# Four convolution layers in one kernel: the stores of x2 move from SyncE's DMA queue to GpSimd's

## The chip, the cores and the metric

One core of one Trainium2 chip runs the whole kernel. The metric is the device time of one execution in microseconds; 2562.26 is the median of three runs before the change.

The core's engines each run their own list of instructions in order: TensorE (PE, matrix products into PSUM), VectorE (DVE), ScalarE (ACT), GpSimd (POOL) and SyncE (SP). A DMA is issued by an engine's list, here SP's or POOL's, and then runs beside the engines. An instruction that waits holds up everything behind it in its own list.

## The reference

The input x is 16 images of 64 channels of 128 x 128 float32. Four layers follow each other, and each adds to its input what it makes of the input's group norm (32 groups of two channels, over the image):

```
x = x + L0(gn(x))    # gram = xf xf^T / N per image; y = gram xf; 1x1 convolution
x = x + L1(gn(x))    # Scharr: |horizontal 3x3| + |vertical 3x3|, each channel for itself
x = x + L2(gn(x))    # a quarter of the channels one column left, a quarter right; 3x3 conv; + b
x = x + L3(gn(x))    # 3x3 conv, 1x1 conv, batch norm over all images, leaky relu, clip to 0..255
```

In the kernel's names x2 is the result of L1's line, the input of the third layer; x3 is the result of L2's line; y is what L3's convolutions give ahead of the batch norm. The batch norm needs sums over all 16 images, so y or x3 of every image is kept in DRAM and the output is made in a second pass.

## The kernel before

**Tiles.** An image lies in SBUF as 128 partitions: 64 channels times two halves of the rows. It is worked in NS = 8 chunks of R = 8 rows for each half. The constants and the order are at lines 16 to 82.

**Stages of an image.** `Gram` (line 557) reads the image by columns (`xr` tiles, 512 KB a load, on SP), copies it on ACT into `xw` and makes the Gram matrix on PE; a chain of small steps (`gram_chain`, line 387) gives the mixing matrix `abd`. `Front` (line 624) loads x (`load`, line 639: one half on SP's queue, one on POOL's), multiplies it by `abd` on PE into `po`, writes the normalized rows with ACT into `xh` (three chunks in turn), and makes the Scharr layer in `scharr` (line 736). `Layer2` (line 889) loads x2 back with the shifted columns into `v` tiles (`load`, line 897: even rows on SP's queue, odd rows on POOL's, six to twelve DMAs a chunk), normalizes them in place on ACT (`norm`, line 957), takes the row differences on DVE into `dA` or `dB`, and multiplies on PE into the PSUM pair `two`, which DVE empties into x3 (`combine`, line 1022). `Layer3` (line 1042) does the like from x3 to y. The x3 and y stores are on SP's queue (lines 884 and 1123). For odd chunks POOL also copies half of `dB` to the tile `q2` with two DMAs (line 939).

**The x2 tile and its buffers.** `scharr` writes in place: the tile `u` (line 739, tag "u", two buffers from the pool `work`) becomes the x2 chunk after six parts, named in `SCHARR` (line 24): "stencil", "smooth", "slope", "abs" (ACT), "x +" and "+ y". The first DVE instruction of a chunk, the one in "stencil", overwrites the buffer of the chunk two before. So it has to wait until that chunk has been read by its store and by ACT's square sum (line 727).

**The store.** `Front.store` (line 766) writes a chunk of x2 to the DRAM tensor `x2_d` in two DMAs, one for the even and one for the odd rows of each half. Each takes 128 partitions x 4 rows x 128 values: 512 pieces of 512 bytes, 256 KB. Both are issued by `sp`. It is called in the part "x2" of the next chunk's step (line 724). The eighth chunk's store is what the next stage's first `v` load of the same image waits for.

**Order.** A step handles one chunk of `Front` and one pair of chunks of `Layer2` or `Layer3`; several images are in work at a time. Inside a step the parts come in the order of the table `ORDER` (line 27), one list for each kind of step. `InOrder` (line 124) keeps the instructions in program order, so each engine's list is the table written out. In SP's list a pair of x2 stores stands between loads of `v`, x and `xr` and stores of x3 and y. POOL's list has its halves of the x and `v` loads, the `q2` copies, the small steps of the norm coefficients (`rstd`, line 340, and `coefficients`, line 356), a few memsets (lines 715 and 720) and, at the end, the stores of the output.

**Semaphores.** The framework gives each kind of queue eight completion semaphores in turn. A DMA waits for the one eight before it on its queue to have landed.

**The second pass.** From about 2010 us no x2 is made any more: y or x3 is loaded, the batch norm applied, and the output stored (lines 1351 to 1456).

Of the kernel before, what the change touches and what calls it, by code (L numbers as in the profile page):

```python
# [170 lines left out]
def tile_kernel(ctx: ExitStack, tc: tile.TileContext, x, cw_h, w2_t, b2, wbin_t, w1_t, b1, gamma, beta, consts, out):  # L171
    nc = tc.nc
    pe, dve, act, sp, pool = (InOrder(tc, e) for e in (nc.tensor, nc.vector, nc.scalar, nc.sync, nc.gpsimd))
# [38 lines left out]
    def planes(d):  # L212

        return d[W:W + 2 * C * PLANE].rearrange("(p s j w) -> p s j w", s=2, j=NP // 2, w=W)
# [409 lines left out]
    class Front:  # L624
# [141 lines left out]
        def store(self, i):  # L766
            d = planes(x2_d[self.b])
            for s in range(2):
                sp.dma_start(
                    d[:, s, i * R // 2:(i + 1) * R // 2, :],  # L770
                    self.x2[i].rearrange("p (j s) w -> p s j w", s=2)[:, s],
                )
# [722 lines left out]
```

## Time and profile before

| | |
|---|---|
| runs | 2562.26 us median of 3 (2558.72 to 2563.32) |
| profiled execution | 2563.73 us, of which 2562.0 is the span from the first to the last instruction |
| granted TensorE clock | 0.976 in the mean |
| HBM | 321.46 MB read, 243.28 MB written |
| DMAs issued by SP | 58.0% of 16 DMA engines' time, 425.34 MB |
| DMAs issued by POOL | 20.1%, 156.63 MB |
| x2 stores | 256 DMAs of 256 KB on SP's queue, 4.9 us from issue to landing (median of those whose landing is known) |
| x loads | 128 DMAs of 256 KB on each queue, 4.5 us to landing from SP, 4.9 from POOL |
| one DMA on POOL's engine | `v` loads 503 ns, `q2` copies 524, x loads 602, output stores 537 to 549 |

How to read the profile: it shows one execution. [...] A group of instructions is named "out<-in" by the tiles it writes and reads, buffer numbers left out; so `x_d<-u` is a store of x2, `x_d<-x` a store of x3, and `v<-x_d` a load of x2. All lines are 134 because a helper records each instruction. The time in brackets is the idle time of the engine just before an instruction, with what released it. "SPq" is SP's list. The PSUM pair is `two`, the stencil's tile `u`.

### The profile page before, as it was taken

The page shows a single profiled execution, that of the slowest core. Times are in us where ns is not written, and L with a number is a line of the kernel's source. Part 1 is how long each engine was busy: PE and PEld are TensorE (multiplying, and loading weights), DVE is VectorE, ACT ScalarE, POOL GpSimd, SP SyncE. Part 2 cuts the span into 40 slices and gives each one's busy share as a digit, 9 for nine tenths or more (in the row PEclk, how much of TensorE's full clock was granted, in tenths as well). Part 3 has the DMA queues.
Part 4 walks back from the last instruction along what each step waited for, and adds up shares of the span by engine and source line. Part 5 has one row for each costly group of instructions (what it writes and reads, how often), then busy time and mean ns, then how long its engine had stood idle before and what let it go on. Part 6 is the DMA issues. An engine that isn't in the chain of part 4 may idle for free. (4 is left out here: it accounts for less than half of the span.)

```text
span 2562.0 us, 52738 instructions
## 1 busy us (share of the span) xinstructions
PE 2425.1 (95%) x19286; PEld 938.8 (37%) x19286; DVE 2120.4 (83%) x2939; ACT 2029.4 (79%) x3253; POOL 698.8 (27%) x1254
## 2 busy tenths in 40 slices
PE   6587999999999999999999999999999999999996
PEld 5332333333333333434343434343333333333332
DVE  4999999999999999999999999999999634444333
ACT  4777888889797979797978888887888655787775
POOL 3241313131313132323232323232321310222222
PEclk8688999999999999999999999999999999999998
DMA  9776979796767676757576979776767688999998
GB/s 228 194 195 180 233 199 233 192 233 188 191 171 193 163 197 160 201 160 201 160 199 173 243 192 231 200 205 168 200 170 193 156 264 261 417 417 417 413 412 338
DMA packets 610577, 585.33 MB, mean 228 GB/s; under 512 B 48480, under 2 KB 521984, under 8 KB 610320
## 3 DMA queue, kind: packets, MB, share of 16 engines
q1 hardware_dynamic: 556752, 425.34, 58.0%
q0 software_dynamic: 53568, 156.63, 20.1%
q8 instruction: 153, 2.51, 0.4%
q14 instruction: 104, 0.85, 0.1%
HBM read 321.46 MB, written 243.28 MB: 220 GB/s over the span
## 5 line engine op out<-in xcount | busy, mean ns | idle before, releaser
L134 PE MATMUL two<-dA,w 64*64 64x512 f32 (+2 forms) x2304 | 533.9, 595 | 0.0
L134 PE MATMUL two_again<-v_again,w 64*64 64x508 f32 (+1 forms) x3456 | 376.6, 592 | 10.7 <-ACT v_again L134 10.7
L134 POOL DMA_DIRECT2D v<-x_d x480 | 238.8, 503 | 499.8 <-PE one L134 220.3
L134 PE MATMUL one<-v,w 128*64 128x508 f32 (+2 forms) x1600 | 360.8, 584 | 0.3 <-ACT c L134 0.3
L134 PE MATMUL one<-v,wi 128*64 128x508 f32 (+3 forms) x1536 | 346.8, 585 | 13.6 <-ACT c L134 13.5
L134 PE MATMUL two<-dB,w 64*64 64x512 f32 (+2 forms) x1536 | 353.5, 593 | 0.0
L134 DVE SCALAR_TENSOR_TENSOR e<-e 128x1032 f32<-128x1032 f32 (+1 forms) x256 | 313.4, 1224 | 0.0
L134 ACT ACTIVATE xh<-po,co 128x128 f32<-128x128 f32 (+1 forms) x480 | 274.1, 619 | 13.3 <-PE po L134 12.4
L134 PEld LDWEIGHTS two<-dA,w 64*64 64x64 f32 (+1 forms) x2304 | 148.9, 133 | 276.9 <-issue 269.3
L134 ACT ACTIVATE junk<-x 128x1024 bf16<-128x1024 f32 x128 | 134.9, 1054 | 117.0 <-DVE x L134 116.5
L134 PEld LDWEIGHTS two_again<-v_again,w 64*64 64x64 f32 x3456 | 131.7, 134 | 254.7 <-issue 227.9
L134 ACT ACTIVATE v<-v,co 128x1154 f32<-128x1154 f32 x128 | 171.8, 1343 | 60.7 <-DMA v<-x_d 58.9
L134 ACT ACTIVATE v<-x,co 128x1024 f32<-128x1024 f32 (+3 forms) x256 | 205.0, 846 | 3.8 <-POOL co L134 3.8
L134 PE MATMUL po<-x,abd 64*64 64x512 f32 (+1 forms) x1024 | 183.3, 621 | 23.7 <-ACT xh L134 18.4
L134 DVE SCALAR_TENSOR_TENSOR u<-xh 128x1170 f32<-128x1170 f32 x128 | 176.0, 1375 | 34.5 <-DMA x_d<-u 28.1
L134 DVE SCALAR_TENSOR_TENSOR y<-two,c 128x1024 f32<-128x1024 f32 x128 | 156.0, 1219 | 52.4 <-issue 20.6
L134 DVE TENSOR_TENSOR dB<-v 128x1024 f32<-128x1024 f32 (+1 forms) x128 | 152.1, 1188 | 39.8 <-ACT v L134 31.9
L134 PEld LDWEIGHTS one<-v,w 128*64 128x64 f32 x1600 | 107.5, 137 | 206.2 <-issue 170.1
L134 PEld LDWEIGHTS one<-v,wi 128*64 128x64 f32 x1536 | 102.8, 136 | 215.7 <-issue 159.4
L134 ACT ACTIVATE junk<-y 128x1024 bf16<-128x1024 f32 x128 | 135.1, 1055 | 55.0 <-DVE y L134 53.7
L134 PE MATMUL two<-q,cross 64*64 64x512 f32 (+1 forms) x768 | 169.6, 570 | 6.3 <-issue 5.7
L134 PE MATMUL two<-dA,wi 128*64 128x508 f32 (+1 forms) x768 | 175.0, 589 | 0.0
(228 smaller groups left out, 4253.5 us busy)
## 6 DMA issues: line engine op xcount, KB each, us to landing
x_d<-u SPq DMA_DIRECT2D x256, 256.0 KB, 4.9
x_d<-x SPq DMA_DIRECT2D x490, 128.0 KB, 3.7
xr<-in_x SPq DMA_DIRECT2D x120, 512.0 KB, 6.2
y_d<-y SPq DMA_DIRECT2D x320, 128.0 KB, 3.8
x<-in_x SPq DMA_DIRECT2D x128, 256.0 KB, 4.5
x<-in_x POOLq DMA_DIRECT2D x128, 256.0 KB, 4.9
end_x<-x_d SPq DMA_DIRECT2D x36, 512.0 KB, 17.5
xw<-x_d SPq DMA_DIRECT2D x33, 512.0 KB, 17.2
```

Of the source, the lines that this page charges most:

```text
L134: return self.tc.keep_in_program_order(call(*args, **kwargs))
```

## The change

The two DMAs of each x2 chunk are issued by POOL's list instead of SP's. They stand at the same place of the program, in the part "x2"; shape, source and destination are as before. 256 DMAs go from one list to the other.

```diff
@@ -766,7 +766,7 @@
         def store(self, i):
             d = planes(x2_d[self.b])
             for s in range(2):
-                sp.dma_start(
+                pool.dma_start(
                     d[:, s, i * R // 2:(i + 1) * R // 2, :],
                     self.x2[i].rearrange("p (j s) w -> p s j w", s=2)[:, s],
                 )
```

## The prediction

> **What bounds the kernel now.** I read the engines' shares and the forty slices first, to find the stages.
>
> ```profile
> PE 2425.1 (95%) x19286; PEld 938.8 (37%) x19286; DVE 2120.4 (83%) x2939; ACT 2029.4 (79%) x3253; POOL 698.8 (27%) x1254
> ...
> PE   6587999999999999999999999999999999999996
> ...
> POOL 3241313131313132323232323232321310222222
> ```
>
> PE is full from the fifth slice (256 us) on, and POOL is never busier than four tenths. Then I cut the run where each image's eighth x2 chunk is finished on DVE, and asked for busy times: ten images together (380.28 to 1644.26), image 9 alone, image 13 alone.
>
> ```profile
> core 0: us, PE busy (x) PEld busy (x) DVE busy (x) ACT busy (x) POOL busy (x), PEclk, DMA share, GB/s
> 380.28:1644.26 1263.98, 1241.91 (x9844) 487.89 (x9842) 1215.89 (x1711) 1074.25 (x1792) 366.00 (x656) 1.00 0.74 194
> 1139.50:1265.81 126.31, 124.18 (x988) 48.79 (x986) 121.58 (x172) 107.42 (x181) 37.10 (x66) 1.00 0.69 181
> 1644.26:1768.58 124.32, 123.08 (x988) 48.49 (x986) 121.49 (x173) 102.41 (x176) 35.89 (x65) 1.00 0.69 183
> ```
>
> In the ten images PE idles 1263.98 - 1241.91 = 22.1 us, 2.2 each; DVE idles about 4.8 each. So PE bounds the middle with DVE close behind: DVE can lose only some 2.6 us an image (124.2 - 121.6) before PE feels it. Image 13 idles 1.24 on PE. What is different there shows in the waits.
>
> ```profile
> POOL v L134 <- DMA x_d<-u: 92.6, 16, 7.1
> ...
> ACT v L134 <- DMA v<-x_d: 58.9, 32, 3.5
> ...
> DVE dB L134 <- ACT v L134: 31.9, 18, 8.7
> DVE u L134 <- DMA x_d<-u: 28.1, 12, 3.2
> ```
>
> The columns are total us, times, longest. The last row is the x2 store itself: twelve times DVE may not write a `u` buffer because the store two chunks back has not landed. These twelve lie at 64, 193, 319, 572 and then once an image up to 1581, always at the fifth chunk, 1.5 to 3.2 us; images 3 and 13 to 15 have none. Why is that store late? SP's order of time in image 9 (a program line's "x_d<-u" is a pair of x2 stores, "x_d<-x" are x3 stores):
>
> ```profile
> 1188.29 5.69 SPq L134 DMA_DIRECT2D xr<-in_x  x3
> 1194.07 3.98 SPq L134 DMA_DIRECT2D x_d<-u  x2
> 1198.16 5.90 SPq L134 DMA_DIRECT2D x_d<-x  x8
> 1204.37 2.67 SPq L134 DMA_DIRECT2D v<-x_d  x6
> ```
>
> DVE ended that chunk's x2 at 1185.31, yet SP stood in three 512 KB `xr` loads until 1194 and needed 3.98 us to issue the pair. Then DVE, PE and ACT:
>
> ```profile
> 1200.71 0.22 DVE L134 SCALAR_TENSOR_TENSOR co<-av,co 128x1 f32<-128x1 f32 x1
> 1203.59 1.38 DVE L134 SCALAR_TENSOR_TENSOR u<-xh 128x1170 f32<-128x1170 f32 x1 [2.66 <-DMA x_d<-u]
> ...
> 1206.66 1.23 DVE L134 SCALAR_TENSOR_TENSOR x<-two,c 128x1024 f32<-128x1024 f32 x1
> ```
> ```profile
> 1208.00 0.65 PE L134 MATMUL two<-q,cross 64*64 64x512 f32 x2 [0.80 <-issue]
> ```
> ```profile
> 1210.64 1.35 ACT L134 ACTIVATE v<-v,co 128x1154 f32<-128x1154 f32 x1 [1.55 <-DMA v<-x_d]
> ```
>
> DVE lost 2.66 us, so it emptied the PSUM pair `two` only at 1207.9; PE, which refills it, started 0.80 late at 1208.00. ACT meanwhile waited 1.55 for the last `v` load, whose SP half went out at 1204.37, and DVE lost another 0.64 to that at 1213.11.
>
> **The change, part by part.** Removed from SP: 256 DMAs, 0.36 to 3.85 us each, and SP's own wait for DVE ahead of them. Added to POOL: 256 DMAs of 128x4x128, 512 pieces of 512 bytes each.
>
> *Price of one on POOL.* No row of POOL has 512 pieces. Its x loads with 64 pieces take 538 ns (14 of them before 170 us), with 128 pieces 611 ns (112 after 200 us): 73 ns for 64 more. Six steps more than the second would be 611 + 6 x 73 = 1.05 us. Bounds: 0.52 us (the q row, as if pieces cost nothing) to 4 x 0.611 = 2.44 us (as if they cost everything). I take 1.05, since the two rows give a slope: 256 x 1.05 = 269 us, POOL 699 to 968 us (133 to 625 more by the bounds).
>
> *What hides it.* I laid the pairs into POOL's order as the changed program has it, beside the times of before in image 9. Chunk 0's pair follows the `v` loads at 1156.6, chunk 1's those at 1172.1, chunk 2's those at 1188.4 and chunk 3's an x load at 1204.2; each x2 is done by then (1155.04, 1170.34, 1185.31, 1200.80), and POOL's next job with a deadline comes 7.2, 7.6, 7.0 and 1.5 us later. Chunks 4 and 5 wait for DVE at 1219.31 and 1235.20 inside gaps that last to 1222.08 and 1242.22. At 2.1 us a pair only x loads, three chunks ahead of use, and a memset move, by 0.6 to 2 us: nothing. At 4.9 us a pair the x loads and one memset an image move by 3 to 4 us; still nothing on PE.
>
> *A step that is moved behind something.* Chunk 7's pair stands ahead of the next image's first `v` load, which already waits for that store today (the POOL row above, 16 times). The pair lands later: on SP it was issued at 1265.84 and let POOL go at 1268.46. In the five images from 634 on, 256 KB x loads land 4.4 us after issue from POOL and 3.8 from SP, so 0.6 later plus 0.1 to 2.1 of issue: 1 to 3 us. That first `v` is normalized at 1285.41, and its load lands by about 1273; the cover is some 12 us. Price 0; without cover, 16 x 1 to 3 = 16 to 48 us.
>
> [...] POOL's DMA rows spread little (484 to 620 ns for `v`) although DVE is 96% busy beside them. [...]
>
> *What is gained.* Chunk 2's pair starts near 1188.9 instead of 1194.07 and SP loses 3.98 us of work before the x3 stores and the last `v` load. The store then lands by about 1196 (1188.9 + 2.1 + 4.9, the store row's median), DVE wants the buffer at 1200.9: the 2.66 goes. But DVE now wants the last `v` 2.66 sooner, and gains only if that load too comes sooner; SP is 3 to 4 us ahead, so mostly yes. The nearest row for "no wait for the store" is image 13: 1.24 idle, with 1.40 us of DVE wait for `v` still in it. Ten images: 22.1 - 10 x 1.24 = 9.7 us. Bounds: 0 (the `v` wait takes all of it) to 22.1 - 10 x 0.35 = 18.6 (0.35 is the stall 27 us into each image, where PE waits for an ACT eviction). I take 9.7.
>
> *Elsewhere.* Image 1 (132.90 to 255.40) is DVE's, with a 2.29 store wait: half, 1 us gained (0 to 2.3). Images 14 and 15: DVE never waits for the store; 0. From 2010 on there are no x2 stores; 0. Loss: moved transfers beside SP's loads, two ACT waits for `v` an image. I charge 2 us in all (0 to 20, below).
>
> Sum: -9.7 - 1 + 2 = -8.7. The profiled execution took 2563.73 (span 2562.0 and 1.7 around it); it would be 2555.0. It is 1.5 over the median of the runs shown (2562.26), so the median goes to 2553.6: **2554**.
>
> **The rivals.** *The wait is replaced* (2561, or 2558 to 2564). DVE comes to `dB` 2.66 us early and waits for ACT's `v` instead of for the store. For it: 0.64 already stands there, and 1.40 in image 13. Against: SP's six `v` issues wait behind exactly the stores that go. Gain 1 us.
>
> *Everything goes* (2543). PE falls to 0.35 idle an image: 18.6 gained. Against: image 13 did not get there.
>
> *POOL's queue crowds SP's loads* (2582; slower). A pair is 524 KB; at 417 GB/s, the highest slice, it holds the 16 engines 1.26 us, at the 181 of image 9 2.9 us. If it runs while SP's half of a `v` load is on its way, ACT's normalization is late by as much, and DVE too once ACT's slack is used. One hit an image: 16 x 1.26 = 20 us, up to 46. It decides as soon as the last `v` of an image lands later than today's 1210.6. For it: POOL's packets are larger (10560 for 27.64 MB, against SP's 139690 for 85.58 MB in five images). Against: SP issues that `v` 3 to 4 us earlier, and the bytes are the same. [...]
>
> **How the numbers follow.** Forecast 0.45 (own range 2546 to 2560), replaced 0.22, everything 0.08, crowded 0.25. The range takes in "everything" and the low part of "crowded": 2543 to 2576, which leaves some 0.15 above and 0.05 below. A measurement of this kernel tells about 0.2%, 5.1 us, from no change. Faster: 0.38 of the forecast, all of "everything", 0.02 of "replaced" = 0.48. Within: 0.06 + 0.17 + 0.01 = 0.24. Slower: 0.24 + 0.03 + 0.01 = 0.28.
>
> **What would show it.** The POOL row for x2 stores near 1.05 us, POOL at some 970 us; the row DVE `u` <- x2 store gone; PE's idle of the ten images near 12 us; SP's last `v` issue of an image 3 us closer to the chunk's start; the first `v` normalized at the same place in its image. I am wrong if POOL's price is over 2.4 us, if ACT's wait for `v` grows past 59 us in total, or if DVE's wait only changes its name.

## The result, and the profile after

The changed kernel takes 2568.46 us (median of 7 runs, 2566.26 to 2570.76) where the kernel before, beside it, took 2560.08 (2558.72 to 2563.32): a ratio of 1.0029, 95% interval 1.0019 to 1.0039. A second comparison gave 1.0012 (1.0004 to 1.0021). It is slower by 3 to 8 us. The prediction said 2554.

The first part of the page and two groups of GpSimd (POOL in the profile), after:

```profile
PE 2420.2 (94%) x19286; PEld 934.0 (36%) x19286; DVE 2119.8 (83%) x2939; ACT 2029.9 (79%) x3253; POOL 899.0 (35%) x1510
```
```profile
L134 POOL DMA_DIRECT2D v<-x_d x480 | 239.5, 505 | 211.8 <-ACT e L134 65.2 <-PE one L134 43.1 <-DMA x_d<-u 18.7
L134 POOL DMA_DIRECT2D x_d<-u x256 | 197.7, 776 | 487.7 <-DVE u L134 437.8 <-DVE gs L134 37.4 <-issue 6.5
```

A store costs GpSimd 776 ns, 198 us in all, and its `v` loads cost what they did (505 ns, 503 before). GpSimd's busy time has these rows in it: it is 200.2 us longer than before (899.0 and 698.8). So GpSimd is not short of time. The waits (total us, times, longest):

```profile
DVE dB L134 <- ACT v L134: 63.0, 21, 8.3
...
ACT v L134 <- DMA v<-x_d: 47.9, 21, 7.0
...
ACT v L134 <- DMA x_d<-u: 22.6, 6, 5.6
...
ACT v L134 <- DMA x_d<-x: 20.2, 4, 5.8
POOL v L134 <- DMA x_d<-u: 18.7, 14, 2.1
```

DVE's wait for the x2 store (28.1 us before) is gone. Two rows stand for it: DVE's wait for ACT's `v` has doubled (31.9 before), and ACT's waits for `v` loads, under three names, sum to 90.7 (58.9 before). Busy times of the ten images, of image 9 and of image 13, with the columns of the prediction's windows:

```profile
381.92:1650.86 1268.94, 1239.99 (x9842) 485.85 (x9840) 1215.27 (x1712) 1073.94 (x1792) 489.85 (x816) 0.99 0.74 193
1143.38:1271.45 128.07, 124.48 (x986) 48.76 (x984) 121.56 (x172) 107.33 (x181) 48.98 (x82) 0.99 0.70 178
1650.86:1775.10 124.24, 123.17 (x988) 48.55 (x986) 121.47 (x172) 102.39 (x176) 48.96 (x81) 1.00 0.70 184
```

The ten images are 5.0 us longer; PE idles 29.0 us in them instead of 22.1. In image 9, SP's list, GpSimd's, and then DVE, ACT and PE, in order of time:

```profile
1192.10 6.49 SPq L134 DMA_DIRECT2D xr<-in_x  x3
1198.68 9.61 SPq L134 DMA_DIRECT2D x_d<-x  x8
1208.61 2.69 SPq L134 DMA_DIRECT2D v<-x_d  x6
```
```profile
1205.29 3.04 POOL L134 DMA_DIRECT2D v<-x_d  x6
...
1208.91 1.68 POOL L134 DMA_DIRECT2D x_d<-u  x2
```
```profile
1204.98 1.37 DVE L134 SCALAR_TENSOR_TENSOR u<-xh 128x1170 f32<-128x1170 f32 x1
...
1218.76 0.96 DVE L134 TENSOR_TENSOR dB<-v 128x768 f32<-128x768 f32 x1 [4.91 <-ACT v L134]
```
```profile
1216.30 1.35 ACT L134 ACTIVATE v<-v,co 128x1154 f32<-128x1154 f32 x1 [5.84 <-DMA x_d<-x]
```
```profile
1224.81 1.94 PE L134 MATMUL one<-v,wi 128*64 128x512 f32 x6 [3.25 <-ACT c L134]
```

The stencil's `u` starts with no wait. But SP reaches its last `v` loads no sooner: counted from the image's start (the end of the eighth x2 chunk, 1143.38 here) the first is issued at 65.2, and at 64.9 before. The 3.98 us that its store pair took is taken by the eight x3 stores behind it, 9.61 us instead of 5.90. And while SP's `v` loads are on their way, GpSimd sends chunk 3's pair (1208.91). Counted from the trace's packets, in the stretch from 64 to 71 us of images 3 to 12, KB an image:

| queue | before | after | after, chunk 3 on SP (below) |
|---|---|---|---|
| GpSimd's | 496 | 1039 | 511 |
| SP's | 1152 | 910 | 1075 |

GpSimd's queue carries 543 KB more there, about one pair of stores (524 KB), and SP's 242 KB less. The last `v` is normalized at 1216.30, 72.9 us into the image (71.1 before); DVE, early now, waits 4.91 for it.

**What an image's length hangs on.** Image 9 cut at the start of that `dB`, before:

```profile
1139.50:1213.11 73.61, 72.47 (x620) 28.62 (x618) 69.57 (x93) 59.78 (x109) 26.41 (x51) 1.00 0.75 193
1213.11:1265.81 52.70, 51.72 (x375) 20.17 (x372) 52.01 (x79) 47.64 (x73) 10.69 (x15) 1.00 0.61 163
```

and after:

```profile
1143.38:1218.76 75.38, 75.03 (x668) 30.06 (x666) 69.56 (x94) 59.78 (x109) 34.78 (x62) 1.00 0.74 192
1218.76:1271.45 52.69, 49.44 (x320) 18.70 (x318) 52.00 (x79) 47.55 (x73) 14.20 (x20) 0.97 0.63 158
```

Behind `dB` both take 52.7 us, DVE busy in 52.0 of it, although PE idles 0.98 in the one and 3.25 in the other. PE's stall costs nothing; DVE has hardly any slack from there on. With the 2.46 us from the start of the normalization to `dB`, an image lasts until the last `v` is normalized, and 55.18 us more. That holds in eleven of the thirteen profiles of this study to 0.07 us in the mean of ten images (the exceptions: 55.33 and 55.51), as the sixth column of the table shows.

| kernel | median us | ratio to before, 95% interval | last `v` normalized, us into the image | ten images, us | behind that, us an image | last DRAIN, us |
|---|---|---|---|---|---|---|
| before | 2560.08 | | 71.21 | 1263.99 | 55.19 | 7.09 |
| after | 2568.46 | 1.0029 (1.0019, 1.0039) | 71.67 | 1268.94 | 55.23 | 9.95 |
| after, again | 2568.16 | 1.0012 (1.0004, 1.0021) | 71.66 | 1268.36 | 55.18 | 9.95 |
| third `u` buffer, stores on SP | 2564.28 | 1.0000 (0.9991, 1.0009) | 71.24 | 1264.19 | 55.18 | 7.09 |
| chunk 3 on SP | 2555.35 | 0.9966 (0.9954, 0.9978) | 70.64 | 1258.17 | 55.18 | 4.03 |
| chunk 3 on SP, ahead of `v` | 2582.93 | 1.0073 (1.0060, 1.0086) | 72.25 | 1274.25 | 55.17 | 4.24 |
| chunk 3 on GpSimd, late | 2559.53 | 0.9984 (0.9975, 0.9992) | 70.63 | 1258.10 | 55.18 | 10.60 |
| chunk 3 on ACT | 2564.03 | 0.9999 (0.9991, 1.0007) | 71.00 | 1265.12 | 55.51 | 4.11 |
| only chunk 3 on GpSimd | 2579.04 | 1.0054 (1.0041, 1.0067) | 72.62 | 1278.12 | 55.19 | 9.70 |
| last two images on SP | 2563.96 | 1.0003 (0.9991, 1.0015) | 71.81 | 1269.89 | 55.18 | 4.59 |
| after, `xr` spread | 2535.10 | 0.9886 (0.9873, 0.9900) | 68.00 | 1233.28 | 55.33 | 9.95 |
| before, `xr` spread | 2530.39 | 0.9869 (0.9856, 0.9883) | 68.53 | 1237.36 | 55.21 | 7.09 |
| after, `xr` spread, chunk 3 on SP | 2528.63 | 0.9864 (0.9851, 0.9877) | 68.27 | 1235.13 | 55.25 | 4.12 |

Columns four and six are means over images 3 to 12 of one profiled execution, column five is their sum; column six is a tenth of column five less column four. The kernel before measured 2560.08 to 2564.56 beside the different rows, so rows are compared by their ratios. "Last DRAIN" is the last long DRAIN of GpSimd's list, at the end of the program, from the trace's records.

**Where the time went,** in the profiled executions (spans 2562.0 and 2569.0): to the first image's eighth x2 chunk -1.3; images 1 and 2 +3.0; images 3 to 12 +4.9; images 13 to 15 -2.0; the second pass up to the DRAIN -0.4; the DRAIN +2.9 (7.09 to 9.95). The sum is +7.0 with the parts unrounded. Images 1 and 2 scatter: they took 250.4 us in this profile and 256.2 in the second one of the same changed kernel (the longest of its twelve runs), so their +3.0 is not shown to be the change's. The ten images and the DRAIN came out nearly the same in both (1268.9 and 1268.4; 9.95).

### The profile page after: what moved, and what is told of

Read it like the earlier page. It is cut to its first block, busy times and chain, and to the rows that moved or that the text cites. A ratio compares the mean times of both kernels' runs of the same rounds, so it can differ in the third digit from the quotient of the medians.

```text
span 2569.0 us, 52715 instructions
## 1 busy us (share of the span) xinstructions
PE 2420.2 (94%) x19286; PEld 934.0 (36%) x19286; DVE 2119.8 (83%) x2939; ACT 2029.9 (79%) x3253; POOL 899.0 (35%) x1510
## 5 line engine op out<-in xcount | busy, mean ns | idle before, releaser
L134 PE MATMUL one<-v,wi 128*64 128x508 f32 (+3 forms) x1536 | 355.0, 597 | 29.4 <-ACT c L134 29.3
L134 POOL DMA_DIRECT2D x_d<-u x256 | 197.7, 776 | 487.7 <-DVE u L134 437.8
L134 POOL DMA_DIRECT2D v<-x_d x480 | 239.5, 505 | 211.8 <-ACT e L134 65.2
L134 PE MATMUL po<-x,abd 64*64 64x512 f32 (+1 forms) x1024 | 176.1, 624 | 23.8 <-ACT xh L134 21.2
L134 POOL DMA_DIRECT2D q<-dB x128 | 68.8, 539 | 321.8 <-issue 212.9
```

Of the source, the lines that this page charges most:

```text
L134: return self.tc.keep_in_program_order(call(*args, **kwargs))
```

## The experiments

**The wait alone.** The kernel before, with a third buffer for `u`.

```diff
-                self.u = work.tile([P, R + 1, W + 2], F32, tag="u", name=f"u_{self.b}_{i}")
+                self.u = work.tile([P, R + 1, W + 2], F32, tag="u", name=f"u_{self.b}_{i}", bufs=3)
```

> The kernel before (all x2 stores on SP), with a third buffer for u, so that DVE's 28.1 us wait for the x2 store is gone and no transfer changes its queue. If that wait was worth what the prediction said (9.7 us of PE idle), 2548 to 2553. If the last v load ends just behind it (theories A and B both say it lands about 71 us into the image), DVE's wait moves to dB, whose idle time grows from 39.8 to 60-70 us, PE idle of images 3 to 12 stays at 20 to 26 us, and the time is 2556 to 2563. If it comes out at 2566 or more, the loss of the change has nothing to do with the queue but comes from taking the wait away.

Measured: 2564.28 beside 2563.86 for the kernel before, ratio 1.0000; that is just above the range expected.

```profile
L134 DVE SCALAR_TENSOR_TENSOR u<-xh 128x1170 f32<-128x1170 f32 x128 | 175.9, 1375 | 4.6 <-ACT xh L134 4.6
L134 DVE TENSOR_TENSOR dB<-v 128x1024 f32<-128x1024 f32 (+1 forms) x128 | 152.2, 1189 | 71.1 <-ACT v L134 49.8 <-DMA x_d<-x 13.5 <-DMA x_d<-u 7.8
```

DVE's wait for the store is gone (4.6 us before `u`, none of it the store's), `dB`'s idle time is 71.1 us instead of 39.8, the last `v` comes at 71.24. The whole wait moved to the `v`: it was worth nothing. PE's idle rose to 29.2, above what was expected, and cost nothing. So the change's loss isn't the price of an absent wait either.

**Chunk 3 back on SP,** behind the last `v` loads.

```diff
-                pool.dma_start(
+                (sp if i == 3 else pool).dma_start(
```

> The changed kernel, but with chunk 3's pair of x2 stores (the pair that GpSimd issues 65.3 us after the image's start, beside SP's last v loads at 64.2 to 67) back on SP's queue, behind those loads. Theory A (the last v load of an image is what ends last, and the x2 stores that now run beside it take DMA time from it): the last v is normalized 1 to 2 us earlier (after: 71.7 us into the image, mean of images 3 to 12), PE idle of images 3 to 12 falls from 28.9 to 15-22 us, median 2553 to 2561. Theory B (SP reaches its last v loads late because it stands in the xr loads, whoever issues the stores): nothing moves, 2565 to 2571. Theory C (GpSimd's issue time, 776 ns a store, delays its own v loads): 32 of 256 stores fewer, at most a tenth of the loss comes back, 2565 to 2570.

Measured: 2555.35, theory A's range; B and C said 2565 or more. The last `v` comes 1.03 us sooner than after the change, and the ten images are 10.8 us shorter. The time is helped by a DRAIN of 4.03 us instead of 9.95, which theory A had not in it. With that one pair out of the way the other seven bring part of what the prediction had hoped for: 5.8 us less than before in these images, where it had 9.7. PE idles 25.1 us, more than the 15 to 22 expected, again to no cost.

**Only chunk 3 on GpSimd,** the mirror image (`pool if i == 3 else sp`).

> The kernel before, with chunk 3's pair of x2 stores alone on GpSimd's queue (32 of 256 stores): the mirror image of the run with chunk 3 back on SP. Theory A (these two stores run beside SP's last v loads and take DMA time from them): the last v of images 3 to 12 is normalized later than the 71.2 us of before, DVE's wait for v at dB grows by over 10 us (39.8 before), and the time is 2566 to 2576, slower than before by 3 to 12 us, although seven eighths of the stores stay where they were. Theory B (who issues the stores is without effect on the last v): within 3 us of before. GpSimd's last DRAIN (7.09 us before, 9.95 after, 4.03 with chunk 3 on SP) may add or take up to 3 us.

Measured: 2579.04, above the range that theory A gave. One eighth of the change does more harm than the whole: the last `v` comes at 72.62. In the mean of the ten images SP issues the last of its six `v` loads at 68.4 us instead of 67.2, and that is most of the 1.4 us. Chunk 2's pair stays ahead of these loads on SP and chunk 3's now runs beside them, which would explain it, but this was not tried by itself. `dB`'s idle time is 50.4 (+10.6), the DRAIN 9.70 (+2.6).

**Queue or order?** Chunk 3's pair on SP, once behind the last `v` loads as above and once just ahead of them. For that its call moves to the end of its own step, and in that step "load b" behind it.

```diff
+                if i == 3 and part == "+ y":
+                    self.store(3)
...
+        names = list(ORDER[kind_of(step)])
+        if any(step - FIRST - NS * b == 3 for b in fronts):
+            names.remove("load b")
+            names.insert(names.index("+ y") + 1, "load b")
```

> As the run with chunk 3's pair on SP, but with this pair issued just ahead of SP's last v loads instead of just behind them: the same queue, the same bytes, only the order of two neighbours on SP changed. Theory A says that the loss comes from 512 KB that go ahead of the last v load on busy DMA engines, whichever queue carries them: the last v of images 3 to 12 is normalized 1 to 3 us later than the 70.6 us of that run, and the time goes from 2555.4 to 2565-2580. If GpSimd's queue as such were the cause, the order on SP would not matter much: 2553 to 2560.

Behind (image 9 starts at 1136.59), SP and then ACT:

```profile
1201.85 2.73 SPq L134 DMA_DIRECT2D v<-x_d  x6
1204.68 1.38 SPq L134 DMA_DIRECT2D x<-in_x  x1
1206.17 1.08 SPq L134 DMA_DIRECT2D x_d<-u  x2
```
```profile
1207.64 1.35 ACT L134 ACTIVATE v<-v,co 128x1154 f32<-128x1154 f32 x1 [4.21 <-DMA v<-x_d]
```

Ahead (image 9 starts at 1149.12):

```profile
1213.13 1.12 SPq L134 DMA_DIRECT2D x_d<-u  x2
1214.57 2.98 SPq L134 DMA_DIRECT2D v<-x_d  x6
```
```profile
1222.18 1.35 ACT L134 ACTIVATE v<-v,co 128x1154 f32<-128x1154 f32 x1 [6.22 <-DMA v<-x_d]
```

In this image the `v` loads go out at nearly the same place, 65.26 and 65.45 us into it; the last `v` is normalized at 71.05 and at 73.06. In the mean of the ten images they go out later, though: SP issues the six at 65.7 to 68.6 us instead of 64.6 to 66.9, and the last `v` is normalized 1.61 us later. From the last issue to the normalization it takes 3.60 us instead of 3.75. So two neighbours on one queue, exchanged, are worth 27.6 us of the median (theory A gave 10 to 25), and the kernel is slower than with GpSimd's queue; it takes no second queue to do the harm. But it is done here by SP's later issue, and what the pair's bytes do to a load that is under way this run does not show. The next one does.

**The other way round: on GpSimd, but late.** Chunk 3's pair goes out behind the `q2` copies; `u` has a third buffer.

```diff
                 self.scharr(i, SCHARR.index(part))
+                if i == 4 and part == "+ y":
+                    self.x2[3] = self.late
+                    self.store(3)
+                    self.x2.pop(3)
```

> The changed kernel with chunk 3's pair still on GpSimd's queue, but issued some 12 us later, behind the q copies at 77 us into the image, when the last v load has landed; u gets a third buffer, so that the late store holds up no stencil (a third buffer alone changed the time by 0.0%). Theory A: as good as with chunk 3 on SP behind the loads or a little better, 2549 to 2560, last v at 70 to 71 us; GpSimd's last DRAIN as in the changed kernel (9.95 us), since its list of DMAs has the same length, so rather 2555 to 2562. If the software queue as such delays SP's loads, it stays at 2565 to 2572.

Image 9 starts at 1136.09; GpSimd and ACT:

```profile
1212.10 1.56 POOL L134 DMA_DIRECT2D x_d<-u  x2
```
```profile
1206.78 1.35 ACT L134 ACTIVATE v<-v,co 128x1154 f32<-128x1154 f32 x1 [3.20 <-DMA v<-x_d]
```

Measured: 2559.53. All 256 stores on GpSimd, and the last `v` at 70.63 and ten images of 1258.10 us, as with chunk 3 on SP (70.64, 1258.17). The medians still differ by 4.2 us, the DRAINs by 6.6 (10.60 against 4.03). So GpSimd's queue as such isn't the cause; the place of the pair in time is. From SP's last `v` issue to the normalization it takes 4.56 to 4.70 us in the three profiles in which the pair goes out from GpSimd beside these loads and the other pairs do too (the changed kernel twice, and the control below), and 3.75 to 4.10 in the three in which it goes out behind them (on SP, on ACT, late on GpSimd). The rest of the 1.04 us between early and late is SP's last issue, at 67.1 and at 66.6 us.

**On ACT.** Chunk 3's pair on a third queue (`act if i == 3 else pool`).

> The changed kernel, with chunk 3's pair on ACT's queue, where program order puts it behind ACT's normalization of the last v: neither on GpSimd's queue nor on SP's, but again behind the last v load in time. Theory A: what counts is that it starts after that load has landed, so as with chunk 3 on SP: 2552 to 2559, last v normalized at 69.5 to 71 us. If instead SP's FIFO was the benefit (or the store needs SP), it stays at 2564 to 2571.

Measured: 2564.03, a miss. The last `v` comes at 71.00, sooner than the changed kernel's 71.67, so the direction is theory A's. But behind it images 5 to 8 last 55.51 to 56.53 us, where the other six keep to 55.17 to 55.21. ACT's queue takes 0.37 and 0.53 us for the pair in image 9, and ACT stands 0.47 us before its next instruction; whether this makes the longer images was not tried by itself.

**A control: 32 other stores on SP,** those of the last two images (`sp if self.b >= 14 else pool`).

> The changed kernel, with the x2 stores of the last two images (again 32 of 256) on SP: a control for the run with chunk 3 on SP, with as many stores taken off GpSimd but not those beside the last v load of images 2 to 13. Theory A: images 3 to 12 stay as in the changed kernel (PE idle 27 to 30 us, last v normalized near 71.7), and if GpSimd's last DRAIN depends on how many DMAs it issued, it is 4.03 us instead of 9.95 and the time falls by just that, to 2560 to 2565. If the DRAIN stays at 9.95: 2566 to 2571. If it reaches 2553 to 2558, any 32 stores off GpSimd would do, and theory A falls.

Measured: 2563.96. The last `v` (71.81) and the ten images (1269.89) stay where the changed kernel has them, so it isn't enough to take any 32 off GpSimd. The DRAIN falls to 4.59 us, 5.4 less, and the ratio from 1.0029 and 1.0012 to 1.0003, 2 to 7 us. The twelve runs spread over 13 us (2558.88 to 2572.22) and the profiled one, 2571.71, is among the longest.

**The `xr` loads spread.** Of three 512 KB loads that SP issues at 49 to 51 us into an image, two come between 69 and 73, behind the last `v` loads; once in the changed kernel, once in the kernel before.

```diff
-            if i == 1 and q == 0:
-                for m in range(3):
-                    self.load(m)
+            if 4 * i + q in (4, 9, 10):
+                self.load({4: 0, 9: 1, 10: 2}[4 * i + q])
```

> The changed kernel, with the first three xr loads of an image (512 KB each, on SP at 49 to 51 us into the image) spread: one stays, two come at 69 and 73 us, behind the last v load. Theory A and B both say that the stretch from 46 to 70 us, in which the 16 DMA engines are 90 to 117% busy, loses 1 MB, the last v is normalized 2 to 5 us earlier, PE idle of images 3 to 12 falls from 28.9 to about 10-15 us and the time to 2548 to 2556. A theory in which GpSimd's own issue time or order is the cause says no change, 2565 to 2571. If the xr loads come too late for their use at 82 to 98 us, a new stall of ACT's xw copy shows there.

> The kernel before with the same move of two xr loads, x2 stores on SP. SP no longer stands in the xr loads when chunk 2's store is due (194 us... issued 54.6 us into the image before, 9 us after it was ready), so DVE's wait for the store falls from 28.1 to under 8 us and the last v loads are issued some 3 us earlier. Theory A and B: 2546 to 2554, and no slower than the changed kernel with the same move by more than 3 us. If the x2 stores on SP are better even then because FIFO order behind the v loads protects these (theory A), it is faster than that kernel; if SP's issue is the limit (theory B), it is slower than that kernel.

Measured: 2535.10 and 2530.39, each 33 us below the same kernel without the move, where 6 to 20 had been expected. SP, in the kernel before with that edit (image 9 starts at 1117.67):

```profile
1166.45 0.42 SPq L134 DMA_DIRECT2D xr<-in_x  x1
1167.90 1.37 SPq L134 DMA_DIRECT2D x_d<-u  x2
...
1179.91 2.65 SPq L134 DMA_DIRECT2D v<-x_d  x6
```

The last `v` loads go out at 62.2 us (61.2 in the mean of ten images, 64.9 before) and chunk 2's pair at 50.2 instead of 54.6, on SP. So theory B was half right: what SP stands in sets when the `v` loads go out, and the move is worth more than all that the stores do. It also takes 1 MB out of that stretch; the two were not tried apart, but the last `v` comes 2.7 us sooner and its loads are issued 3.7 us sooner, so the issue alone would cover it. The comparison of the two was to tell A from B and did not: the one with stores on SP is 4.7 us faster, but in images 3 to 12 it is 4.1 longer; it is ahead in images 1 and 2 (242.6 against 247.0 us) and in the DRAIN (7.09 against 9.95). Why images 1 and 2 gain was not followed up; in two profiles of the changed kernel they differ by 5.8 us. (In the second text "194 us... issued 54.6 us" should read 54.6 us only.)

**Both helps.**

> Both helps together: two xr loads behind the last v load, and chunk 3's pair on SP, the rest of the x2 stores on GpSimd. With the xr loads spread, PE idles only 0.35 to 0.8 us an image, so theory A leaves little for chunk 3 to win in the images: 0 to 3 us. GpSimd's last DRAIN should be 4.03 us instead of 9.95, as the list of its DMAs has the same length as in the run with chunk 3 on SP. Together 2526 to 2532, against 2535.1 with only the loads spread and 2530.4 with the loads spread and all x2 stores on SP. If it stays above 2533, the DRAIN is not set by the list of GpSimd's DMAs.

Measured: 2528.63, ratio 0.9864, with a DRAIN of 4.12 us: the best, though its interval overlaps that of the `xr` loads spread alone in the kernel before (0.9869). Once these loads are out of the way, it matters little who issues the stores. The other half of the last `v`, GpSimd's, is a likely reason: it is issued at 61.7 us and lands at 67.7 in the mean in the kernel before, where the last `v` is normalized at 71.21, and at 67.8 here, where that is at 68.27.

**The changed kernel again,** beside the two kernels on order.

> The changed kernel itself, beside the two runs above on the same chip, to compare them with. As measured before: ratio 1.003 to the kernel before, 2566 to 2572; PE idle of images 3 to 12 27 to 31 us, last v normalized near 71.7 us, GpSimd's last DRAIN 9.95 us again if it is set by the program and not by chance.

Measured: 2568.16 and a ratio of 1.0012, lower than the 1.003 expected, as the kernel before stood at 2564.56 there. Last `v` 71.66, DRAIN 9.95, as the first time; PE idle 31.4.

## Why the prediction was wrong, point by point

- **What bounds the middle: wrong.** It read PE's fuller row as the bound, "with DVE close behind", and priced waits by PE's idle time. The windows behind `dB` and the table's 55.18 show a chain through DVE that is closed once an image by the last `v`. PE idled 22.1, 25.1 and 29.2 us in kernels whose ten images took 1264.0, 1258.2 and 1264.2.
- **DVE's wait for the x2 store: read rightly, priced wrongly.** It fell away as said. Alone it is worth 0 (third buffer), the lower of the two bounds that stood beside the 9.7.
- **The step that failed: "SP is 3 to 4 us ahead, so mostly yes".** The last `v` loads were issued at 64.7 us instead of 64.9 in the mean of the ten images. In image 9 the next DMAs of SP's list took the time that the stores gave up (9.61 us for eight x3 stores).
- **The term that turned the sign: "I charge 2 us in all" for moved transfers beside SP's loads.** Chunk 3's pair beside the last `v` loads costs 10.8 us in the ten images alone (1268.94, against 1258.17 with that pair on SP behind them), and the other pairs bring 5.8 instead of 9.7. The bounds, 0 to 20, had the 10.8 within them; the sum took the low end. The 1 us of image 1 can't be judged, as the scatter of images 1 and 2 is larger.
- **GpSimd's price: right in kind, too high.** 776 ns a store against 1.05 us estimated (bounds 0.52 to 2.44), 198 us against 269. POOL came to 899 us, 968 foreseen. The stores' rows spread as little as those of the `v` loads: 750 to 837 ns a store in the whole execution, with DVE busy for 96% of the ten images, and 484 to 612 ns a `v` load (484 to 620 before).
- **"What hides it": true of GpSimd's own work, and it looked at the wrong thing.** GpSimd's last `v` loads go out at the same place, 61.65 us in most images of both kernels. What was not asked is what the pair, going out at 65.5 instead of 68.8 in image 9, runs beside.
- **Chunk 7's pair ahead of the next `v`: right, 0.** GpSimd's wait for it fell from 92.6 to 18.7 us, and nothing shows behind it: the first `v` of image 9 is normalized 19.59 us into it in both kernels.
- **The rivals.** "The wait is replaced" is what the third buffer shows by itself (2564.28 against 2563.86). On top of that comes "POOL's queue crowds SP's loads". Its place (the last `v`) and its sign were right. Its price was 1.26 us an image; the pair costs 1.03 (70.64 against 71.67), but the other pairs that leave SP give 0.6 back, and both together are far from its 2582. Its reason, the queue with its larger packets, is not what decides: late on the same queue the pair costs nothing (70.63), and SP's own queue does worse (72.25) in the wrong order. Whether the larger packets made the early pair dearer was not tried.
- **Not thought of at all:** the DRAIN at the end, 2.9 of the 7.0 us of the profiled executions.

## What to carry to other kernels

Before pricing a wait, find what closes the loop: cut the repeating stretch at each candidate event and see after which one its length no longer varies; the fullest engine need not be it, and a stall on it may cost nothing, as PE's 3.25 us in image 9 did here. Moving the stores to another queue moved their bytes in time (543 KB an image more on GpSimd's queue from 64 to 71 us); of any such move ask which load the bytes will stand ahead of in a list, or run beside, since two neighbours exchanged on one queue cost more here (27.6 us) than any change of queue. A queue that gives up an issue is not ahead by that time if its next DMAs are then slower to issue, as the x3 stores were here (9.61 us for eight instead of 5.90).

## What the runs showed of the hardware that was not expected

GpSimd's last DRAIN goes with the list of DMAs that it issued: 7.09 us in the three profiles with 926, 9.70 with 958, 4.03 to 4.59 in the five with 1150, 9.95 to 10.60 in the four with 1182. It does not rise with the number. Nor is it the wait for the last store: in all thirteen profiles the last DMA has landed 2.9 to 3.2 us after the DRAIN's start. What sets it stays open.

In the ten images of the changed kernel the clock granted to PE was halved five times, for 3.41 us each (6.83 in image 4), beside five of PE's six longest stalls: from within the stall in images 4 and 7, from 0.4 to 0.9 us behind it in the others. Two windows of the changed kernel in image 7, around the end of a stall of 3.00 us (the clock is the third value from the end):

```profile
968.80:972.80 4.00, 2.82 (x8) 0.99 (x10) 4.00 (x6) 4.00 (x8) 1.53 (x2) 0.62 0.80 240
972.80:976.80 4.00, 4.00 (x18) 0.99 (x16) 3.82 (x7) 2.67 (x6) 0.20 (x1) 0.95 1.03 264
```

These stalls lasted 4.18, 3.00, 3.25, 1.96 and 1.93 us (images 4, 7, 9, 11 and 12); beside one of 1.94 in image 8 the clock stayed at 1.00, and so it did beside all that were shorter; in the kernel before, with stalls up to 1.55, it stayed at 1.00 in these images. The length of the stall does not settle it: beside 3.08 us the clock stayed at 1.00 in one image of the kernel with chunk 3 on ACT (image 9) and fell in another (image 8). Like the stalls it cost nothing in four of the five: those images still last 55.16 us behind the last `v`. Image 4, with the longest, takes 55.78, and in the kernel with chunk 3 on ACT the two images with a lowered clock (7 and 8) are the two longest.
